# Layer 1's high halves and values stored from ScalarE's queue instead of SyncE's

## The chip, the cores and the metric

The kernel runs on one core of one Trainium2 chip. A core has five engines with instruction streams of their own: TensorE (PE), VectorE (DVE), ScalarE (ACT), GpSimd (POOL) and SyncE (SP). A DMA is issued by an instruction in one of these streams and then carried out by the core's 16 DMA engines. An engine takes its instructions in order, so an instruction that waits for a semaphore holds up all that stand behind it in the same stream. The metric is the device time of one execution in microseconds (us). The runs are given with their median; a profile belongs to one execution.

## The reference, cut to what matters

A network of two layers on x of shape (2, 512, 512), all in float32. Both layers have the form

```python
h = _layernorm(x) * (1 + ca) + sa
x = x + ga * attention(h)
h = _layernorm(x) * (1 + cb) + sb
x = x + gb * ffn(h)
```

Layer 0's attention is a chunked linear attention with decay (32 heads of 128, 8 key heads, chunks of 128 rows), with an RMS norm, a silu gate and an output projection; its FFN is a product with a matrix of signs, scaled. Layer 1's attention is what the change touches:

```python
xq = (x @ wq + bq).reshape(B, S, 32, 16)
xk = (x @ wk + bk).reshape(B, S, 8, 16)
xv = (x @ wv + bv).reshape(B, S, 8, 16)
q, k = _rope(xq, cos, sin), _rope(xk, cos, sin)
k, v = jnp.repeat(k, 4, axis=2), jnp.repeat(xv, 4, axis=2)
scores = jnp.einsum('bqhd,bkhd->bhqk', q, k) / 4
out = jnp.einsum('bhqk,bkhd->bqhd', softmax(scores), v)
```

Layer 1's FFN mixes four streams of 128 by a 4 x 4 matrix per row, which 50 Sinkhorn iterations make doubly stochastic.

## The kernel before

**Precision.** Large products run in three passes: a float32 operand is split into a high half (rounded to the fp32r type) and a low half (the rest), and `passes` (L248 to 255) adds high x high, high x low and low x high in one PSUM tile. The high half is made by a cast on ACT, the low half mostly by a subtraction on POOL, so the low half is always later than the high one.

**Who sets the order.** The kernel's text gives each operation's engine; the order in which each engine runs its instructions is found when the kernel is built, by a scheduler that plays the program through in a model of the timing and takes what is ready by priority (`schedule_with_timeline_sim=True`, L1587). An edit of one queue can so move instructions on all engines. Tiles come from pools with a fixed number of buffers, and a new use of a buffer waits for the last reader of the old one. Before the change every DMA of the kernel is issued by SP. Each DMA reports its end on one of eight semaphores, taken in turn; a DMA that takes a semaphore again waits for the earlier DMA on it, eight issues before.

**Stages.** Layer 0 is worked through in 64 units of one key head, batch and chunk. For each unit SP loads a row of decay sums into all partitions (`gb<-g_dram`, L530, one per unit), POOL masks the differences (`dec<-gb`, L532), ACT takes their exponential (L79) and DVE multiplies (L545) them into the scores. Of the rest of a unit these names occur below: `v` (L499) and `xw` (L559) weigh the values, `qh` and `ql` (L490, L491) are the halves of the queries, `yps` (L585) and `z` (L595) the outputs, `gps` and `pps` products with the gate and query weights, whose halves are `wg_h`, `wg_l` and `wq_h`, `wq_l`.

Layer 1 begins for batch 0 while layer 0's units of batch 1 are still running: `tail(n)` (L726 to 763) is called after each unit and does, by the distance c from the batch's last unit, the first norm, layer 0's FFN, the second norm, and at c = 8, 10 and 12 the projections that the change touches. They run at about 818 to 911 us for batch 0 and 1040 to 1079 us for batch 1.

**The stores.** `biased` (L695 to 698) is a projection with its bias, an ACT pass at L697. `rope_halves` (L700 to 713) turns it: `rot` is a shuffle on DVE, the products are on POOL (L705) and DVE (L706), the sum on DVE or POOL; the cast to `hi` is on ACT (L709), the subtraction for `lo` on POOL (L711), and both are stored in DRAM (L713). `project_kv` (L717) does this for the keys and stores the values (L719), `project_q` (L721) for one of four tiles of queries. Each store moves 128 x 512 float32, 256 KB. Per batch there are one value store, a high and a low one of the keys, and four high and four low ones of the queries: eleven stores, 22 in both batches.

**Who reads them.** The detour through DRAM brings the heads into another partition layout. `keys1` (L827 to 836) loads `ks` from `k_dram` (L834), `queries1` (L838 to 854) loads `qs` from `q_dram` (L849), a high row block and a low one, and `values1` (L858 to 871) loads `vT` from `v_dram` (L860), which PE transposes (`vps`, L863). All of these loads are issued by SP and wait for the stores that they read. The scores `s<-ks,qs` (L899) then run on PE, DVE takes the maxima of each row (L903), PE and ACT turn those (L917, L922) and SP writes them as extra rows into `qs` (L923); a second product (L937) gives the shifted scores, ACT their exponential `pt` (L79), and PE the weighted values `op` (L957). Layer 1's gate and norm rows are loaded at L1004 and L1012; L1117 transposes the FFN's input (`xpt`). The Sinkhorn iterations (`iterations`, L1183) run on POOL and DVE and end the kernel.

Of the kernel before, what the change touches and what calls it, by code (L numbers as in the profile page):

```python
# [9 lines left out]
FP = mybir.dt.float32  # L10
# [33 lines left out]
H1, KV1, D1 = 32, 8, 16  # L44
# [9 lines left out]
def tile_adaln(ctx: ExitStack, tc: tile.TileContext, a: dict, out: bass.AP):  # L54
    nc = tc.nc
# [116 lines left out]
    def temp(shape, dt, name, bufs=2):  # L172
        return wk.tile(shape, dt, name=name, bufs=bufs)
# [205 lines left out]
    for kc in range(KC):  # L379
# [13 lines left out]
        out=upto, in_=all1, pattern=[[1, P]], compare_op=ALU.is_ge, fill=0.0, base=0, channel_multiplier=-1,  # L393
# [73 lines left out]
    def project(n, hh, b):  # L467
        hi, lo = W[n, hh]
        ps = bank([P, L], "pps")
        passes(ps, [((hi[:, kc * P:(kc + 1) * P], lo[:, kc * P:(kc + 1) * P]), hcol(b, kc)) for kc in range(KC)])  # L470
        return ps
# [223 lines left out]
    def biased(n, t, i, b):  # L695
        raw = temp([P, L], FP, "raw1")
        nc.scalar.activation(raw, project(n, t, b), AF.Identity, bias=l1c["bias"][:, i:i + 1])  # L697
        return raw

    def rope_halves(n, t, i, b, dst):  # L700

        raw = biased(n, t, i, b)
        rot = temp([P, L], FP, "rot1")
        nc.vector.stream_shuffle(rot, raw, [j ^ 8 for j in range(32)])
        nc.gpsimd.tensor_tensor(raw, raw, l1c["rope"][0], ALU.mult)  # L705
        nc.vector.tensor_tensor(rot, rot, l1c["rope"][1], ALU.mult)  # L706
        (nc.gpsimd if RA else nc.vector).tensor_tensor(raw, raw, rot, ALU.add)
        hi = temp([P, L], FR, "hi1")
        nc.scalar.copy(hi, raw)  # L709
        lo = temp([P, L], FR, "lo1")  # L710
        nc.gpsimd.tensor_tensor(lo, raw, hi.bitcast(FP), ALU.subtract)  # L711
        for src, r in ((hi, 0), (lo, D1)):
            nc.sync.dma_start(out=dst[:, r:r + D1, :], in_=src.bitcast(FP))  # L713

    v_dram = [dram.tile([P, L], FP, name=f"v_dram{b}") for b in range(B)]

    def project_kv(b):  # L717
        rope_halves("wk1", 0, 4, b, k_dram[b])
        nc.sync.dma_start(out=v_dram[b], in_=biased("wv1", 0, 5, b))  # L719

    def project_q(b, t):  # L721
        rope_halves("wq1", t, t, b, q_dram[b][8 * t:8 * t + 8])
# [3 lines left out]
    def tail(n):  # L726
# [4 lines left out]
        for b in range(B):  # L731
# [25 lines left out]
            if c == 8:  # L757
                l1c["there", b] = True
                project_kv(b)
                project_q(b, 0)  # L760
                project_q(b, 1)
            elif c in (10, 12):
                project_q(b, c // 2 - 3)
# [697 lines left out]
    for n, u in enumerate(units):  # L1461
        g, b, c = u["at"]
# [128 lines left out]
```

## Time and profile before

| | us |
|---|---|
| median of three runs | 1349.3 |
| the runs | 1343.13, 1349.3, 1351.8 |
| the profiled execution | 1342.29 |
| its span | 1340.5 |
| stores of layer 1, batch 0, on SP | 818.3 to 911 |
| stores of layer 1, batch 1, on SP | 1049 to 1079 |

The span is the time between the first and the last instruction of the profiled execution; 1.8 us lie around it. The mean granted clock of PE was 0.969 of full speed.

The page gives the busy time of each engine and then cuts the span into 40 slices of 33.5 us; each digit is the busy share of a slice in tenths, and 9 stands for 90% or more. The row PEclk is the clock that PE was granted. In the groups of instructions each row has a line of the kernel, an engine, an operation, output and inputs, the count, the summed busy time, the mean of one in ns, and the idle time of the engine just before with what ended it:

```profile
L903 DVE TENSOR_REDUCE m<-s 128x1 f32<-128x512 f32 x256 | 165.7, 670 | 12.4 <-PE s L899 11.8
L532 POOL TENSOR_SCALAR_AFFINE_SELECT dec<-gb 128x512 f32<-128x512 f32 x64 | 47.0, 734 | 93.3 <-DMA gb<-g_dram 46.0
L254 PE MATMUL gps<-wg_h,hh 128*128 128x512 f32 x256 | 101.0, 395 | 0.7 <-DVE st L574 0.7
```

DMA-issuing instructions are not counted as busy; they appear in the timeline as rows of the queue that issues them (SPq for SP). A view of waits lists, for each engine and line, what it waited for, the time in total, how often and the longest.

All DMAs of the execution moved 109.68 MB, a mean of 82 GB/s, and one queue carried nearly all of it:

```profile
q1 hardware_dynamic: 69640, 108.21, 26.6%
q8 instruction: 57, 0.93, 0.3%
q14 instruction: 65, 0.53, 0.1%
```

The columns are packets, megabytes, and the time of the packets as a share of the 16 engines' span. The issues of the stores themselves, by line (ns minimum, median and maximum, then the first and last start in us):

```profile
L713 SPq DMA_DIRECT2D q_dram<-hi x8: 577/586/625, 832.3 to 1076.8; - x8
L713 SPq DMA_DIRECT2D q_dram<-lo x8: 575/588/620, 834.8 to 1078.4; - x8
L713 SPq DMA_DIRECT2D k_dram<-hi x2: 626/662/697, 819.2 to 1052.7; - x2
L719 SPq DMA_DIRECT2D v_dram<-raw x2: 338/340/343, 818.3 to 1049.0; - x2
```

### The profile page before, as it was taken

To read this page: it belongs to the slowest core of one execution; us is meant where nothing else is said; L and a number is where in the kernel's file an instruction comes from. 1 tells how busy PE (TensorE), PEld (TensorE's weight loads), DVE (VectorE), ACT (ScalarE), POOL (GpSimd) and SP (SyncE) were. 2 spreads that over 40 slices of the span, in tenths; PEclk is the share of its full clock that TensorE was granted. 3 is DMA by queue.
4 is the path that set the end of the run, shared out by engine and by line. 5 is a ranking of instruction groups with operands and counts; after the bars stand their busy time and mean duration, and the time that the engine had idled before them with its cause. 6 is when DMAs were issued, how large, how long until landed. Compare 5 with 4: busy or idle time off the path is not lost. (4 is left out here: it accounts for less than half of the span.)

```text
span 1340.5 us, 23011 instructions
## 1 busy us (share of the span) xinstructions
PE 1227.8 (92%) x7216; PEld 990.3 (74%) x7216; DVE 1090.6 (81%) x2665; ACT 842.1 (63%) x2375; POOL 790.9 (59%) x1233
## 2 busy tenths in 40 slices
PE   6999999999999999999989999898999999995508
PEld 3787887888788788888877788676777777764408
DVE  7888678777686687877989887877879889898888
ACT  4666665476466466766657675665758678775417
POOL 4446564364265367676788888535435856668751
PEclk9999999999999999999999999998999999998659
DMA  8013331231132143332343233424214221200001
GB/s 258 27 35 110 110 95 40 71 104 55 53 99 85 55 151 94 93 97 95 103 127 110 67 123 89 125 85 129 83 30 124 76 75 50 66 16 2 9 8 48
DMA packets 69762, 109.68 MB, mean 82 GB/s; under 512 B 13436, under 2 KB 20348, under 8 KB 69640
## 3 DMA queue, kind: packets, MB, share of 16 engines
q1 hardware_dynamic: 69640, 108.21, 26.6%
q8 instruction: 57, 0.93, 0.3%
q14 instruction: 65, 0.53, 0.1%
HBM read 99.89 MB, written 8.02 MB: 80 GB/s over the span
## 5 line engine op out<-in xcount | busy, mean ns | idle before, releaser
L903 DVE TENSOR_REDUCE m<-s 128x1 f32<-128x512 f32 x256 | 165.7, 670 | 12.4 <-PE s L899 11.8
L79 ACT ACTIVATE pt<-s 128x512 f32<-128x512 f32 x256 | 137.8, 601 | 12.2 <-PE s L937 11.2
L484 POOL TENSOR_TENSOR q<-xcos,rot 128x512 f32<-128x512 f32 x64 | 95.7, 1495 | 36.6 <-DVE xcos L482 32.9
L79 ACT ACTIVATE sg<-sg 128x512 f32<-128x512 f32 x128 | 80.9, 632 | 55.5 <-DVE sg L515 53.6
L899 PE MATMUL s<-ks,qs 96*128 96x512 f32 x256 | 103.7, 433 | 9.3 <-DVE m L903 7.5
L79 ACT ACTIVATE dec<-dec,room 128x128 f32<-128x128 f32 x256 | 82.9, 398 | 43.2 <-POOL dec L532 43.0
L254 PE MATMUL pps<-hh,wq_h 128*128 128x512 f32 x256 | 102.2, 399 | 0.8 <-DVE zl L608 0.8
L532 POOL TENSOR_SCALAR_AFFINE_SELECT dec<-gb 128x512 f32<-128x512 f32 x64 | 47.0, 734 | 93.3 <-DMA gb<-g_dram 46.0
L254 PE MATMUL ops<-wo_h,zl 128*128 128x512 f32 x256 | 100.9, 394 | 1.0 <-DVE zl L608 0.9
L254 PE MATMUL ops<-wo_h,zh 128*128 128x512 f32 x256 | 101.2, 396 | 0.7 <-DVE zl L608 0.7
L254 PE MATMUL gps<-wg_h,hh 128*128 128x512 f32 x256 | 101.0, 395 | 0.7 <-DVE st L574 0.7
L937 PE MATMUL s<-qs,ks 100*128 100x256 f32 x512 | 98.8, 299 | 1.9 <-ACT pt L79 1.4
L254 PE MATMUL gps<-wg_l,hh 128*128 128x512 f32 x256 | 100.5, 393 | 0.0
L254 PE MATMUL pps<-hl,wq_h 128*128 128x512 f32 x256 | 100.3, 392 | 0.0
L254 PE MATMUL pps<-hh,wq_l 128*128 128x512 f32 x256 | 100.2, 391 | 0.0
L254 PE MATMUL ops<-wo_l,zh 128*128 128x512 f32 x256 | 100.1, 391 | 0.0
L254 PE MATMUL gps<-wg_h,hl 128*128 128x512 f32 x256 | 100.1, 391 | 0.0
L595 DVE SCALAR_TENSOR_TENSOR z<-yps,ss,sg 128x128 f32<-128x128 f32 x256 | 71.8, 340 | 31.1 <-ACT ss L79 30.7
L552 POOL TENSOR_TENSOR gb<-gb,q 128x512 f32<-128x512 f32 x48 | 63.8, 1331 | 55.6 <-ACT gb L79 46.4
L585 PE MATMUL yps<-v,dec 128*128 128x128 f32 x512 | 93.0, 277 | 3.1 <-DVE xcos L482 2.8
L937 PEld LDWEIGHTS s<-qs,ks 100*128 100x128 f32 x512 | 82.2, 193 | 18.2 <-ACT pt L79 5.4
L559 POOL TENSOR_TENSOR xw<-v,room 128x512 f32<-128x512 f32 x48 | 57.2, 1205 | 64.7 <-ACT v L499 61.8
(331 smaller groups left out, 3901.7 us busy)
## 6 DMA issues: line engine op xcount, KB each, us to landing
gb<-g_dram SPq DMA_DIRECT2D x64, 256.0 KB
raw<-in_wq SPq DMA_DIRECT2D x56, 256.0 KB
raw<-in_wg SPq DMA_DIRECT2D x48, 256.0 KB
raw<-in_wo SPq DMA_DIRECT2D x48, 256.0 KB
raw<-in_wmod SPq DMA_DIRECT2D x40, 256.0 KB
qs<-q_dram SPq DMA_DIRECT2D x64, 64.0 KB
raw<-in_wk SPq DMA_DIRECT2D x14, 256.0 KB
raw<-in_wv SPq DMA_DIRECT2D x14, 256.0 KB
```

The costliest lines, as they stand in the source:

```text
L79: ins = nc.scalar.activation(o, i, func, **kw)
L254: nc.tensor.matmul(ps, lhsT=l, rhs=r, start=i == 0, stop=i == n - 1)
L484: nc.gpsimd.tensor_tensor(dst, sp(xc_), sp(rot), ALU.add)
L532: anchor["pool"] = nc.gpsimd.affine_select(out=dec, in_=gb, pattern=[[0, REP0], [1, P]], compare_op=ALU.is_ge, fill=-1e30, base=0, channel ...
L552: nc.gpsimd.tensor_tensor(gb, gb, q[:, c], ALU.mult)
L559: nc.gpsimd.tensor_tensor(xw, u["v"][:, c, :].unsqueeze(1).to_broadcast(sh4), wdc[:, c, r0:r0 + REP0].unsqueeze(2).to_broadcast(sh4), ALU. ...
L585: nc.tensor.matmul(yps[:, h, :], lhsT=u["pr"][:, h, :], rhs=u["v"][:, c, :], start=True, stop=not c)
L595: nc.vector.scalar_tensor_tensor(z[:, h, :], yps[:, h, :], ss[:, h:h + 1], sg[:, h * P:(h + 1) * P], ALU.mult, ALU.mult)
L899: anchor["pe"] = nc.tensor.matmul(ps, lhsT=st["qs"][rp][0:KS, i, qt * P:(qt + 1) * P], rhs=st["ks"][s][0:KS], start=True, stop=True,).ins
L903: anchor["dve"] = nc.vector.tensor_reduce(st["m"][:, 2 * qt + s, i:i + 1], ps, AX.X, ALU.max, negate=True).ins
L937: nc.tensor.matmul(ps[:, j, :], lhsT=st["ks"][s][0:KM, kt * P:(kt + 1) * P], rhs=st["qs"][rp][0:KM, i, :], start=True, stop=True,)
```

## The change

The stores of the high halves and of the values are issued by ACT. The low halves stay with SP, and so do all loads.

```diff
@@ -709,14 +709,14 @@
         nc.scalar.copy(hi, raw)
         lo = temp([P, L], FR, "lo1")
         nc.gpsimd.tensor_tensor(lo, raw, hi.bitcast(FP), ALU.subtract)
-        for src, r in ((hi, 0), (lo, D1)):
-            nc.sync.dma_start(out=dst[:, r:r + D1, :], in_=src.bitcast(FP))
+        for src, r, queue in ((hi, 0, nc.scalar), (lo, D1, nc.sync)):
+            queue.dma_start(out=dst[:, r:r + D1, :], in_=src.bitcast(FP))
 
     v_dram = [dram.tile([P, L], FP, name=f"v_dram{b}") for b in range(B)]
 
     def project_kv(b):
         rope_halves("wk1", 0, 4, b, k_dram[b])
-        nc.sync.dma_start(out=v_dram[b], in_=biased("wv1", 0, 5, b))
+        nc.scalar.dma_start(out=v_dram[b], in_=biased("wv1", 0, 5, b))
 
     def project_q(b, t):
         rope_halves("wq1", t, t, b, q_dram[b][8 * t:8 * t + 8])
```

Of the 22 stores twelve move: per batch the values, the keys' high half and four high halves of queries.

## The prediction

> **What bounds the kernel now.** I read the page's busy times first, then its slices, then the waits of TensorE (PE), then the timeline of each engine around PE's longest wait. Busy times and slices:
>
> ```profile
> PE 1227.8 (92%) x7216; PEld 990.3 (74%) x7216; DVE 1090.6 (81%) x2665; ACT 842.1 (63%) x2375; POOL 790.9 (59%) x1233
> PE   6999999999999999999989999898999999995508
> DVE  7888678777686687877989887877879889898888
> PEclk9999999999999999999999999998999999998659
> ```
>
> PE is the bound up to slice 36. The last four slices (1206 to 1340 us) are the tail of Sinkhorn passes, where DVE is busy 117.59 of 134 us and PE 66.92. The changed stores are issued between 818 and 1078 us. So the question is how early PE gets through its work; the tail then follows as it stands. PE's idle time by stretch (window, its length, PE busy; after the five engines the granted clock):
>
> ```profile
> 838.00:871.00 33.00, 29.33 (x130) 22.19 (x131) 28.93 (x53) 20.20 (x57) 17.86 (x16) 1.00 0.43 124
> 871.00:904.50 33.50, 30.65 (x169) 25.67 (x169) 25.48 (x56) 20.44 (x58) 11.99 (x12) 1.00 0.27 87
> 918.00:923.10 5.10, 0.10 (x1) 0.00 (x0) 3.65 (x4) 5.10 (x12) 4.10 (x4) 0.98 0.34 96
> 923.10:930.00 6.90, 5.94 (x21) 4.70 (x22) 6.68 (x13) 4.37 (x10) 2.62 (x5) 0.52 0.57 167
> 1049.00:1080.00 31.00, 28.41 (x194) 22.52 (x192) 28.93 (x67) 20.70 (x51) 25.16 (x37) 0.94 0.40 109
> 1080.00:1206.00 126.00, 125.41 (x1157) 93.36 (x1159) 112.05 (x347) 99.41 (x245) 75.94 (x313) 1.00 0.18 48
> ```
>
> Idle in these from 838 to 1080: 3.67 + 2.85 + 5.00 + 0.96 + 2.59 = 15.1 us. After the 5 us stop the clock is 0.52 for 6.90 us: 6.90 x 0.48 = 3.3 us more lost. So some 18.4 us is all that better timing could win near these stores. What ended the waits of PE and of SyncE (SP):
>
> ```profile
> PE s L899 <- DVE m L903: 7.5, 5, 5.0
> PE vps L863 <- DVE rot L476: 2.5, 1, 2.5
> PE xpt L1117 <- ACT raw L697: 1.9, 1, 1.9
> SPq L713 <- ACT ss L79: 12.8, 1, 12.8
> ```
>
> The last is 12.8 us in which SP's queue stood behind one store of a high half, up to 905.7. The timelines say what that cost (start, duration, engine and line; in brackets the idle time):
>
> ```profile
> 905.71 0.62 SPq L713 DMA_DIRECT2D q_dram<-hi  x1
> 909.78 0.80 SPq L849 DMA_DIRECT2D qs<-q_dram  x2
> 910.62 0.62 SPq L713 DMA_DIRECT2D q_dram<-lo  x1
> 911.34 0.39 SPq L530 DMA_DIRECT2D gb<-g_dram  x1
> 916.45 0.64 POOL L532 TENSOR_SCALAR_AFFINE_SELECT dec<-gb 128x512 f32<-128x512 f32 x1 [4.17 <-PE ztp L603]
> 917.12 1.28 ACT L79 ACTIVATE dec<-dec,room 128x128 f32<-128x128 f32 x4 [8.71 <-POOL dec L532]
> 923.13 0.79 PE L899 MATMUL s<-ks,qs 96*128 96x512 f32 x1 [5.03 <-DVE m L903]
> ```
>
> The high half was stored at 905.71, the query load behind it waited until 909.78, the low half went at 910.62 and only then the decay rows gb at 911.34. gb landed some 5.1 us later (916.45 on POOL, idle for 4.17 us); ACT (8.71 us idle), then DVE and PE followed, PE at 923.13 with 5.03 us lost. The releaser named for PE is only the last link.
>
> **The change, part by part.** It removes twelve issues from SP and adds twelve on ACT's queue; arithmetic, bytes and destinations are the same. In a comparison of the two programs' instruction lists the scheduler has also reordered PE's rows of about 836 to 930, 1053 to 1110 and 1165 to 1200 us; elsewhere the lists agree or shuffle the tail with equal counts.
>
> (a) *The gb stop.* In the new list SP no longer waits for this high half. But gb still follows the low half, the same tile's POOL subtraction, which cannot start before the high half's cast. In the old trace the cast ended at 905.69 and the subtraction ran from 907.06 for 1.28 us, behind two POOL multiplications of 2.05 us; the new list puts it ahead of those. So it is ready near 906.3 to 906.9 and gb is issued near 907, not 911.34: 4.4 us earlier. All of PE's 5.03 us can go that way; I take -4.4, bounds -5.0 and 0 (0 if SP is held by another wait). Next late is DVE, busy 3.65 of those 5.10 us, which is why I don't take the full 5. With a stop under 1 us the low clock should mostly vanish: 0 to -3.3, taken -2.0, since 1.9 and 2.5 us waits elsewhere show 0.94 or 1.00 and not 0.52.
>
> (b) *Values, first batch.* PE waited 2.5 us at the value transposes (L863); their load was issued at 833.44, behind a high store at 832.31. The new list has the load right behind the key loads, about 1.5 us earlier. -1.5, bounds -2.5 and 0.
>
> (c) *The issues on ACT.* No ACT-issued DMA is in this trace. Nearest rows: SP's issues of these very stores, median 586 ns x8 (q), 662 x2 (k), 340 x2 (v): 4.7 + 1.3 + 0.7 = 6.7 us. ACT is busy 63% of the span, so most of it lies in idle ACT time: 13 us of 33 idle in 838 to 871. Ends: 0 and 6.7. It is on the path where PE waits for ACT: a store now stands between a layer-1 bias pass (L697) and the products that feed xpt (L1117), where PE already waits 1.9; +0.6 there, and as much again at one or two of the other eleven, +1.5 in all. Below nothing is excluded for the issue itself; its removal from SP is costed in (a), (b) and (d). A store sits right behind its own cast, or behind one to six more ACT instructions, so the wait for its data is short. Each DMA also waits for an older DMA on one of eight shared completion semaphores; those named in ACT's list were finished by the old times (the latest issued at 1068.4 on SP against about 1076), so 0; if one isn't, ACT stands still for one landing, 4 to 6 us by the rows above.
>
> SP's head waited up to 12.8 us while an issue takes 0.6: by these rows, what is at stake is the position in the queue, not the issue. [...]
>
> (d) *Second batch on SP.* The low half stored at 1074.98 stands in the new list ahead of four query loads, issued at 1071.39 before. They go at about 1075.5, 4 us later, and land about 5 us after that, at 1080.5, against the product that reads them at 1078.9. Cost 0 to +2; I take +0.5, as PE has other rows in that stretch to fill in.
>
> (e) *Reordered rows.* Same work, other gaps. This can't be worked out from rows; 0, bounds -8 and +8: the gaps left in 838 to 1080 after (a) and (b), 18.4 - 7.9 = 10.5, could largely close, or one stop like the old one could open (5.0 + 3.3 = 8.3).
>
> Sum: -4.4 - 2.0 - 1.5 + 1.5 + 0.5 + 0 = -5.9 us. The profiled execution took 1342.29 us (1340.5 of span, 1.8 around it), 7.0 below the median of the runs, 1349.3. So 1336.4 for such an execution, and 1343.4 for a median. All three runs lie within 0.7%: a change under 1% (13.5 us) can't well be told from none.
>
> **Rivals.**
> *The wait only passes from hi to lo.* SP stands before the low half instead; the scheduler's order puts the gb load no earlier in fact. For: SP's order keeps lo ahead of gb. Against: the landing wait of the query loads (909.78) is no longer between. Price: terms (a), (b) gone, (c) and (d) left: +2, 1351.
>
> *The gaps close.* Reordering and freed SP close all 18.4 us: 1331. For: by the same view SP stood behind ACT for 9.9, 7.7 and 12.8 us from 804 to 960. Against: the 10.5 us outside (a), (b) have other releasers.
>
> *Slower: ACT in its order becomes what PE waits for.* Place: the stage from 838 to 938, where PE's next operand comes over ACT casts (ACT is busy all 5.10 us of 918 to 923.1). A store queued there before such casts delays them by its 0.6 us, or by a landing if its shared semaphore is still out. It decides once the cast is later than PE's work at hand, as at 923.13: then a stop of 5.0 and a low clock of 3.3, beside 6.7 of issues, and without the gains of (a), (b): +15, 1364. Against: ACT has idle time, and the list shows no semaphore that should be late.
>
> **How the numbers follow.** Forecast 0.40 (own range 1336 to 1349: from all of (a) and (b), 10.8, with 2.5 of (e), to nothing won); wait passed on 0.12; gaps close 0.22; slower 0.26, this high because a new order on four engines can open stops that I can't see in the old trace. The predicted time is the forecast's, 1343. The range goes from 1331 to 1363: it leaves out half of each outer case, 0.11 + 0.13 at most, less what lies between them and the forecast. Faster by over 1% (under 1335.8): the gaps' 0.22 and 0.03 of the forecast's edge, 0.25; slower by over 1% (above 1362.8): 0.26; within: 0.49.
>
> **What would show it.** Right: PE's 5.03 us before L899 gone or under 1 us, no stretch at clock 0.52 near 923, gb issued within 2 us of lo's subtraction, the 12.8 us wait of SP gone or now ending at lo, twelve issues of about 0.6 us on ACT. PE's stretch to 1206 ends some 6 us earlier with an unchanged tail. Wrong: a new PE wait over 3 us between 838 and 930 that ends at an ACT cast or at an ACT-issued store; ACT waiting at L713 for a DMA; the query loads of the second batch late by more than 2 us; or a longer tail.

## The result and the profile after

| | before | after |
|---|---|---|
| median, us (17 runs each) | 1350.02 | 1353.46 |
| lowest and highest | 1342.47, 1352.7 | 1349.41, 1357.1 |
| the profiled execution, its span | 1342.29, 1340.5 | 1357.1, 1355.4 |
| mean granted clock of PE in it | 0.969 | 0.953 |

The ratio is 1.0032, 95% interval 1.0018 to 1.0047: the change costs about 0.3%, where some 0.4% less time had been forecast. The two profiled executions are 15 us apart, far more than the medians. The one of before lies 7.7 us below its median and the one of after 3.6 above; 4.1 of the 15 us arise in the first 120 us, where both kernels have the same instruction lists. So a difference of single profiles is worth something only in one stretch of work, and only if other executions repeat it.

From the page of after (busy time of each engine; the granted clock in 40 slices of 33.9 us; the DMA queue that is new):

```profile
PE 1243.9 (92%) x7216; PEld 1003.3 (74%) x7216; DVE 1089.0 (80%) x2665; ACT 842.3 (62%) x2375; POOL 786.5 (58%) x1233
PEclk9999999999999999999999999988999999997659
q10 hardware_dynamic: 1648, 3.15, 0.8%
```

The counts are those of before. 3.15 MB, twelve stores of 256 KB, are now in a queue of their own. PE has 16.1 us more of busy time for the same 7216 products, which is not more work. At the lower clock products took longer (in E9, below, those of 512 columns follow one another every 0.43 us near 887 us, at half clock, and every 0.23 near 912, at full clock), and the clock was lower: ahead of the tail it is below 9 tenths in two slices, from 881 to 949 us, where before had one. 7.5 of the 16.1 us lie in the stretch shown below.

The issues of ACT by line (ns minimum, median, maximum):

```profile
L713 ACTq DMA_DIRECT2D q_dram<-hi x8: 583/587/595, 837.2 to 1089.8; - x8
L713 ACTq DMA_DIRECT2D k_dram<-hi x2: 601/878/1155, 823.8 to 1063.1; - x2
L719 ACTq DMA_DIRECT2D v_dram<-raw x2: 321/336/352, 823.2 to 1059.4; - x2
```

By these medians the twelve take 7.1 us, against 6.7 forecast. Now the stretch of the old 5 us stop, in the timeline of after:

```profile
916.26 1.29 POOL L711 TENSOR_TENSOR lo<-raw,hi 128x512 fp32r<-128x512 f32 x1 [4.54 <-ACT hi L709]
917.58 0.63 SPq L713 DMA_DIRECT2D q_dram<-lo  x1
918.30 0.41 SPq L530 DMA_DIRECT2D gb<-g_dram  x1
923.78 0.64 POOL L532 TENSOR_SCALAR_AFFINE_SELECT dec<-gb 128x512 f32<-128x512 f32 x1 [3.87 <-DMA gb<-g_dram]
925.64 1.05 POOL L559 TENSOR_TENSOR xw<-v,room 128x512 f32<-128x512 f32 x1
926.64 1.29 POOL L484 TENSOR_TENSOR q<-xcos,rot 128x512 f32<-128x512 f32 x1
927.96 1.14 ACT L490 CAST qh<-q 128x512 fp32r<-128x512 f32 x2 [1.20 <-POOL q L484]
928.62 2.79 DVE L491 TENSOR_TENSOR ql<-q,qh 128x512 fp32r<-128x512 f32 x2 [3.15 <-ACT qh L490]
931.33 1.27 DVE L903 TENSOR_REDUCE m<-s 128x1 f32<-128x512 f32 x2
932.06 0.68 PE L899 MATMUL s<-ks,qs 96*128 96x512 f32 x1 [2.75 <-DVE m L903]
```

gb is issued 0.75 us after lo's subtraction ends. By the clock that is 7.0 us later than before, but PE is 11 us behind in its list here, so gb comes some 4 us earlier against the work. PE's stop went from 5.03 only to 2.75 us: POOL's product q, behind its weighing xw, and ACT's cast of it are late next; DVE stands 3.15 us for that cast, and the maxima m that PE needs are behind its ql.

To see where the time went, each execution is cut at the same products of PE's list. This is the stretch that reaches from 830 to 960 us in before, and inside it the part of before's 860 to 905 (window, length, PE busy and count, weight loads, DVE, ACT, POOL, granted clock, DMA share, GB/s). Before:

```profile
830.00:960.00 130.00, 115.67 (x649) 91.84 (x647) 105.91 (x202) 78.51 (x208) 66.12 (x60) 0.97 0.38 110
860.00:905.00 45.00, 41.12 (x213) 33.02 (x212) 36.41 (x78) 26.69 (x78) 18.54 (x18) 1.00 0.24 73
```

After, at the same products:

```profile
833.80:970.50 136.70, 123.21 (x648) 97.24 (x647) 104.11 (x203) 79.58 (x216) 65.54 (x59) 0.91 0.36 107
864.90:913.70 48.80, 44.29 (x212) 33.34 (x215) 36.58 (x75) 25.13 (x70) 17.61 (x17) 0.90 0.22 68
```

6.7 us more for the same 649 products; idle time is a little less (13.5 against 14.3) and the clock is 0.91 instead of 0.97. More than half of it, 3.8 us, lies in 860 to 905, before the old stop, where before had a clock of 1.00. What PE waited for in this stretch of after (total, times, longest):

```profile
PE s L899 <- DVE m L903: 4.3, 3, 2.7
PE cps L254 <- DVE xcos L482: 3.5, 1, 3.5
PE ops L254 <- DVE dec L545: 2.8, 1, 2.8
```

The last two waits stand in no row of before for this stretch.

### The profile page after: what moved, and what is told of

It reads as the page before. It is cut to its first block, busy times and chain, and to the rows that moved or that the text cites. A ratio compares the mean times of both kernels' runs of the same rounds, so it can differ in the third digit from the quotient of the medians.

```text
span 1355.4 us, 22993 instructions
## 1 busy us (share of the span) xinstructions
PE 1243.9 (92%) x7216; PEld 1003.3 (74%) x7216; DVE 1089.0 (80%) x2665; ACT 842.3 (62%) x2375; POOL 786.5 (58%) x1233
## 3 DMA queue, kind: packets, MB, share of 16 engines
q10 hardware_dynamic: 1648, 3.15, 0.8%
## 4 chain that ended last, share of the span: by engine, by line
PE 63%; DVE 16%; POOL 7%; issue 5%; DMA 4%; ACT 3%; SPq 1%; POOLq 0%; DVEq 0%; ACTq 0%
PE pps L254 15%; PE ops L254 10%; PE gps L254 10%; PE op L957 4%; PE s L937 4%; PE s L899 3%; PE yps L585 3%; PE sps L254 2%; PE yps L587 2%; PE cps L254 2%; PE mps L293 2%; PE ztp L603 1%; DVE m L903 1%; POOL q L484 1%; DVE sinkhorn L1211 1%
## 5 line engine op out<-in xcount | busy, mean ns | idle before, releaser
L79 ACT ACTIVATE pt<-s 128x512 f32<-128x512 f32 x256 | 138.0, 600 | 18.8 <-PE s L937 12.4
L484 POOL TENSOR_TENSOR q<-xcos,rot 128x512 f32<-128x512 f32 x64 | 92.4, 1445 | 40.5 <-DVE xcos L482 39.2
L899 PE MATMUL s<-ks,qs 96*128 96x512 f32 x256 | 104.9, 438 | 6.6 <-DVE m L903 4.6
L559 POOL TENSOR_TENSOR xw<-v,room 128x512 f32<-128x512 f32 x48 | 55.3, 1165 | 62.1 <-ACT v L499 59.3
```

Of the source, the lines that this page charges most:

```text
L79: ins = nc.scalar.activation(o, i, func, **kw)
L484: nc.gpsimd.tensor_tensor(dst, sp(xc_), sp(rot), ALU.add)
L559: nc.gpsimd.tensor_tensor(xw, u["v"][:, c, :].unsqueeze(1).to_broadcast(sh4), wdc[:, c, r0:r0 + REP0].unsqueeze(2).to_broadcast(sh4), ALU. ...
L899: anchor["pe"] = nc.tensor.matmul(ps, lhsT=st["qs"][rp][0:KS, i, qt * P:(qt + 1) * P], rhs=st["ks"][s][0:KS], start=True, stop=True,).ins
```

## The experiments

**Holding an order.** The change does two things at once: it moves twelve issues, and the scheduler makes another order on four engines. To part them, a kernel is built with a stored list of instruction names for each engine; behind the last operation, dependencies that set an order and nothing else are added between neighbours of the list:

```diff
+    traced = {i.name: i for i in nc.cur_bb.bb.instructions}
+    for steps_ in json.loads(zlib.decompress(base64.b85decode(ORDER))).values():
...
+            if last is not None:
+                tc.add_manual_dep(m, last.name, order_only, reason="the order held")
+            last = m
```

The tiles' places in SBUF are laid out anew by each build, so they are a third thing that can differ (2192 of 3819 places moved between before and E1). All ratios below are against runs of the kernel before on the same chip.

### E1 to E4: queue and order apart

Four kernels: the stores on SP or on ACT (the diff of the change), each with the order of before or of after. Where the stores are on the other queue than in the kernel that the order comes from (E2 and E3, later E6, E7 and E15), the twelve stores themselves are not in the stored list, and the scheduler places them.

> Stores on SP as before; the order of each engine's instructions is held, by order-only dependencies, to that of the kernel before. The tiles get other addresses in SBUF (2192 of 3819), since the packing is done anew. Control for the next three. Theory A (the slowdown comes from the new order of instructions): within 0.2% of the kernel before. Theory B (it comes from ACT carrying twelve DMA issues): within 0.2% of before. Theory C (it comes from where tiles lie, since a tile that takes over the place of a stored one waits for the store to land): off by 0.3% or more, either way, because the places are shuffled here and nothing else is.

> Twelve stores on ACT as in the change, but PE, DVE, POOL, and ACT's and SP's other instructions held to the order of before. Theory A: no slower than the control with SP (within 0.2% of it), perhaps faster by up to 0.4% since the stop of 5.0 us before L899 loses its cause on SP. Theory B: slower than the control by 0.3% (3 to 4 us). Theory C: differs from the control by its own places, no sign forecast.

> Stores on SP as before, but all engines held to the order that the changed kernel has. Theory A: slower than before by about 0.3%, like the changed kernel. Theory B: like before. Theory C: no sign forecast.

> The changed kernel with its own order held, other addresses. Theory A and theory B: 0.3% slower than before, like the changed kernel. Theory C: may be anywhere within 0.5%.

| | order of before | order of after |
|---|---|---|
| stores on SP | E1 1349.60, 0.9998 [0.9984, 1.0012] | E3 1355.52, 1.0049 [1.0031, 1.0067] |
| stores on ACT | E2 1345.50, 0.9980 [0.9964, 0.9996] | E4 1353.51, 1.0029 [1.0013, 1.0046] |

The new order costs 0.5% with either queue (E3 less E1, E4 less E2); the queue alone brings 0.2% with either order, which is within the intervals. E1 repeats before and E4 repeats after, so neither holding an order nor the places moved the time measurably. The change is slower for its reordered rows, not for anything that ACT or SP does with the stores.

What kind of time is it? For each execution: the length of the stretch above, PE's idle time in it, the time lost in stretches at half clock, where PE was granted 0.50 (as an estimate, half of PE's busy time there, added up from the records), and the rest.

| order | kernel | length | idle | low clock | rest |
|---|---|---|---|---|---|
| of before | before | 130.0 | 14.3 | 2.9 | 112.8 |
| | E1 | 132.8 | 15.7 | 4.1 | 112.9 |
| | E2 | 131.0 | 13.0 | 5.5 | 112.5 |
| | E6 (below) | 131.0 | 13.0 | 5.5 | 112.5 |
| of after | after | 136.8 | 13.5 | 10.7 | 112.6 |
| | E3 | 138.0 | 15.7 | 9.3 | 113.0 |
| | E4 | 136.1 | 15.2 | 7.3 | 113.6 |
| | E5 (below) | 136.5 | 14.4 | 7.9 | 114.1 |

The means are 131.2 and 136.9: 5.7 us more in the new order, of which 0.7 is idle time, 4.3 low clock and 0.6 the rest. That agrees with the 5.9 us between the medians of E1 and E3. By parts, three executions each (before, E1, E2 against after, E3, E4): 860 to 905 takes 45.5 and 49.1 us, 905 to 960 takes 55.7 and 57.1, what lies ahead 30.1 and 30.8.

### E5 and E9: a subtraction that waits for a store

In the profiles of after, E3 and E4 PE stops for 2.8, 3.7 and 4.3 us at the output projection (`ops`), always for DVE's `dec`. In E4, by the timeline:

```profile
859.64 0.58 SPq L713 DMA_DIRECT2D q_dram<-lo  x1
864.18 0.69 DVE L491 TENSOR_TENSOR ql<-q,qh 128x512 fp32r<-128x512 f32 x1 [3.16 <-DMA q_dram<-lo]
864.79 0.86 DVE L545 SCALAR_TENSOR_TENSOR dec<-sps,room,dec 128x128 f32<-128x128 f32 x3
865.80 0.77 PE L254 MATMUL ops<-wo_h,zh 128*128 128x512 f32 x1 [4.33 <-DVE dec L545]
```

The buffer that ql is written to held a half that was being stored, and it came free only when the store had landed, 4.5 us after its issue. DVE stands there 3.16 us, with the products `dec` behind it that PE needs. In after it is the high half stored by ACT at 862.92, whose semaphore ql waits for, and ql starts at 867.03 (the view names POOL's `w_l`, which ended within 0.1 us of that). In E3 ql waits only 0.58 us; there ACT's cast qh stands first, for a high half that SP stored at 860.86, and DVE waits 3.63 us at a `dec` that comes after it:

```profile
864.85 0.62 ACT L490 CAST qh<-q 128x512 fp32r<-128x512 f32 x1 [2.93 <-DMA q_dram<-hi]
```

So it happens with either queue: in the new order a writer meets a buffer that is still being stored, and what PE needs stands behind that writer. E5 moves ql behind the three dec, E9 further behind zl (L608), which PE needs too (in DVE's list, the stores on ACT as in E4):

```diff
-ql L491, dec L545 x3, ..., zl L608, rot x2, m x3
+dec L545 x3, ql L491, ..., zl L608, rot x2, m x3          (E5)
+dec L545 x3, ..., zl L608, rot x2, m x3, ql L491          (E9)
```

> The changed kernel with its own order held, but one DVE instruction moved: the subtraction that makes ql of the next queries (L491) goes behind the three decay multiplications (L545) that stood after it, near 865 us. Theory A1 (the order costs because ql waits at DVE's head for its buffer, and PE waits for the multiplications behind it): PE's wait before the products ops, 2.8 to 4.3 us, falls under 1 us, the low clock after it goes, and the kernel is 4 to 6 us faster than the changed one with its order held (1353.5), so near 1348. Rival A2 (something else is as late): within 1.5 us of 1353.5.

> As the changed kernel with its order held, but DVE's subtraction for ql (L491) goes further back: behind the decay multiplications, the gate and zl (L608), two rotations and three maxima. Theory A1 (DVE stands still for a stored tile to land, since ql got that tile's place, and the items behind ql are what PE needs): PE's waits at 855 to 870 us fall from 3 to 4 us to under 1.5 in all, the low clock near 885 goes, 5 to 6 us faster than 1353.5: 1347.5 to 1349. Rival A2 (the loss of that stretch has another cause, as moving ql by three places changed nothing): within 1.5 us of 1353.5.

E5: 1356.1, 1.0039 [1.002, 1.0059], no gain on E4. The forecast gain of 4 to 6 us did not come. The wait only passed on to zl, which now stood behind ql, by the timeline of E5:

```profile
861.73 0.58 SPq L713 DMA_DIRECT2D q_dram<-lo  x1
866.12 0.69 DVE L491 TENSOR_TENSOR ql<-q,qh 128x512 fp32r<-128x512 f32 x1 [2.20 <-DMA q_dram<-lo]
867.06 0.74 DVE L608 SCALAR_TENSOR_TENSOR zl<-ztp,room,zh 128x512 fp32r<-128x512 f32 x1
867.86 0.58 PE L254 MATMUL ops<-wo_h,zl 128*128 128x512 f32 x1 [3.09 <-DVE zl L608]
```

E9: 1351.8, 1.003 [1.0012, 1.0047], the ratio of E4 again, although the stop at ops fell from 4.33 to 1.10 us. The stretch got only 0.8 us shorter (135.3 against 136.1), as a half-clock stretch of 6.8 us from 882.8 was still there. Taking the wait away alone is worth nothing that can be measured.

### E13 and E14: the row of short products

That half-clock stretch is in every profile of the new order in which PE's list was not edited: from 887.8 in after (granted 0.50 up to 894.6), 882.4 in E4, 885.2 in E5 and 883.8 in E10, 6.8 us each, 3.4 us in E3. Of the old order's, before, E1 and E8 have none there; E2 and E6 have 3.4 us near 877 to 880 and E7 at 868. What PE runs ahead of it, in E9:

```profile
877.22 0.71 PE L899 MATMUL s<-ks,qs 96*128 96x512 f32 x2
877.77 0.40 PE L937 MATMUL s<-qs,ks 100*128 100x256 f32 x2
878.16 0.51 PE L899 MATMUL s<-ks,qs 96*128 96x512 f32 x1
878.82 0.50 PE L937 MATMUL s<-qs,ks 100*128 100x256 f32 x2 [0.15 <-DVE zl L608]
879.93 1.10 PE L899 MATMUL s<-ks,qs 96*128 96x512 f32 x2 [0.61 <-DVE m L903]
881.05 0.51 PE L937 MATMUL s<-qs,ks 100*128 100x256 f32 x2
881.65 1.09 PE L899 MATMUL s<-ks,qs 96*128 96x512 f32 x2
...
883.44 1.39 PE L899 MATMUL s<-ks,qs 96*128 96x512 f32 x2
```

PE is called busy almost throughout, but each score product L899 has to wait for DVE's maximum of an earlier one (0.67 us, the mean in before). From 877.22 to 883.44 it got through 7 products of 512 columns, 6 of 256 and 2 of 128 (in the row left out), together as much as 10.5 of 512. At full clock long products follow one another every 0.23 us (in E9 near 912), so by an estimate 27 of them fit in these 6.2 us: PE streamed some 0.4 of that. In this part of before's list no more than six score products L899 come between two groups of long ones; in the new order it is ten, one ahead of yps and nine behind it. E13 puts the next twelve long products (the projection of layer 0's values, `wv_h` and `wv_l`, 512 columns) four at a time between them, on top of E9; E14 does it on E4, with ql where it was. In PE's list:

```diff
-yps, L899 x2, L937 x2, L899, L937 x2, L899 x2, L937 x2, L899 x2, ..., ttp, wv x12
+yps, wv x4, L899 x2, L937 x2, L899, L937 x2, wv x4, L899 x2, L937 x2, wv x4, L899 x2, ..., ttp
```

> The order of the changed kernel with ql moved back, and on PE the twelve long products of the values' projection (pps, 512 columns) that followed the row of short products are put between them, four at a time, behind yps and two pairs of L937. Theory D (in the new order the score products L899, whose maxima DVE takes at 0.6 us each, stand in a row with yps, ztp and mt, PE streams only a third of the time there, and the clock falls to half for 6.8 us near 885): the low clock near 885 goes or halves, 3 to 5 us faster than with ql alone moved (1351.8): 1347 to 1349. Rival E (the row is not what lowers the clock, or the products wait for something else): within 1.5 us of 1351.8.

> The same without moving ql. Theory D: the low clock near 885 goes, the wait at ql (2.8 to 4.3 us) stays: 2 to 4 us faster than the changed kernel's order (1353.5), 1350 to 1351.5. Rival E: 1353.5 +- 1.5.

E13: 1349.34, 0.9996 [0.998, 1.0012], level with before. Its PE in the same place:

```profile
877.11 0.48 PE L254 MATMUL pps<-hh,wv_h 128*128 128x512 f32 x1
...
878.11 0.63 PE L899 MATMUL s<-ks,qs 96*128 96x512 f32 x2
...
883.33 0.62 PE L899 MATMUL s<-ks,qs 96*128 96x512 f32 x2
```

A pair of L899 takes 0.62 us at 883.33, against 1.39 at 883.44 in E9: the clock stays up. The same work of the part 860 to 905, in E9:

```profile
861.50:909.10 47.60, 43.84 (x212) 32.42 (x214) 36.57 (x75) 25.25 (x70) 16.95 (x17) 0.92 0.21 69
```

and in E13:

```profile
862.40:905.00 42.60, 39.88 (x212) 29.90 (x214) 36.26 (x74) 24.78 (x68) 16.52 (x16) 1.00 0.24 76
```

5.0 us less, with the clock at 1.00; 4.0 of them are PE's busy time for the same 212 products, 1.0 is idle time. The whole stretch from 830 takes 131.3 us, as in the old order (131.2 on the mean). E14: 1352.45, 1.0027 [1.001, 1.0044]. Its profile has no low clock there either and its stretch is 2.3 us shorter than E4's, but the stop at ops is 2.54 us, and the median is that of E4 within its interval. Only both edits together bring the kernel level with before. Against E2, which has the old order with the same queue (0.9980), 0.16% of the order's 0.49% are left, which is within the intervals. Why E14's gain shows in the profile and not in its median is open.

### E6: which of the reordered places

The order also differs from 1053 to 1110 and 1165 to 1200 us. E6 has the stores on ACT, the order of before up to PE's 4300th instruction, which is behind the stretch above, and then that of after:

```diff
-ORDER: before's lists
+ORDER: before's lists up to PE's instruction 4300, then after's
```

> Stores on ACT; the order of before up to a point behind the first batch's stores (PE instruction 4300 of 5944, between 940 and 1040 us), from there the order of the changed kernel. If the loss lies in the first batch's stretch alone: like stores on ACT with the order of before, 1345.5 +- 1.5. If the second batch's new order costs too: 1347 to 1350.

1350.97, 1.0002 [0.9983, 1.002], between E2 (0.9980) and E4 (1.0029) with intervals that overlap E2's. Its stretch of 830 to 960 takes 131.0 us, as in E2. The trace shows a stop of 1.29 us at `ot` (1076.28) that E2 lacks, and 6.8 us at half clock from 1030.3, where E2 has 3.4 from 1027.9 with the same order there. By matched products, the work of before's 1049 to 1115 us takes 0 to 2.0 us more than in before in the executions that have the old order there (before, E1, E2, E7, E8) and 1.4 to 3.8 us more in nine that have the new one (after, E3 to E6, E9, E10, E13, E14): by the means, an estimate of 1.5 us from single executions. So the first batch carries the larger part; whether the second adds 0.2% or nothing was not settled by the medians.

### E7, E8 and E10: the gb stop by itself

In E2, with the high half on ACT but the old order, gb was issued at 911.95 and PE stopped for 4.86 us: SP stood at the query loads, which wait for that store to land, instead of at the store. What holds gb there is the kernel's own rule: `gated` (L150 to 160) keeps a unit's gb load behind SP's work beside an earlier unit. E7 (ACT) and E8 (SP) lift it for SP and set gb ahead, of the query loads and of the high store; the rest of before's order is held. E10 does the like on E9, ahead of the last low store.

```diff
         for e, m in anchor.items():
-            if e != "free" and m.name not in past:
+            if e not in ("free", "sp") and m.name not in past:
```

> Stores on ACT, the order of before, and one SP instruction moved: the load of the decay rows gb that came after the low half's store (911.95 us in the run without this) goes ahead of the two query loads that wait for a store to land. Theory (the 5 us stop of PE before L899 is made by gb's place in SP's queue): the stop falls under 1.5 us, the low clock after it goes too, 5 to 8 us faster than without it, 1338 to 1341. Rival (another input is as late): at most 1.5 us faster, 1344.

> Stores on SP, the order of before, and the same load of gb moved ahead of the high half's store and the query loads. By the same theory the stop goes without any change of queue: 5 to 8 us faster than with the order of before (1349.6), 1342 to 1345. Rival: at most 1.5 us faster.

> The same, and SP's load of gb goes ahead of the last low half's store of the first batch. If the rest of the 5 us stop, 2.75 us and the low clock behind it, hangs on gb alone: 3 to 5 us faster than the run with ql alone moved. If POOL's other work is as late: at most 1.5 us.

E7: 1343.12, 0.9959 [0.9937, 0.9982]. E8: 1343.78, 0.9949 [0.993, 0.9968]. The timeline of E8:

```profile
899.62 0.33 SPq L530 DMA_DIRECT2D gb<-g_dram  x1
...
922.23 0.72 PE L899 MATMUL s<-ks,qs 96*128 96x512 f32 x2 [0.88 <-DVE m L903]
```

gb goes some 12 us earlier than in before, the stop is 0.88 us, and behind it PE is at half clock for 3.4 us (from 924.3) instead of 6.8. The stretch from 830 takes 126.0 us, against 130.0 in before and 132.8 in E1, with 10.5 us idle and 1.6 lost to the low clock (3.4 in E7, which has a second such stretch at 868). This gain of 0.4 to 0.5% was there all along and needs no other queue; E7 and E8 differ by 0.1%. E8's gain on E1, 0.5%, is what was forecast; E7's on E2 is 0.2%, between the forecast and its rival, and why is open. E10: 1351.68, 1.0026 [1.0007, 1.0046]. Its stop fell only from 2.98 to 2.14 us. In the new order gb is no longer what is late: POOL's next q waits 1.32 us for DVE's xcos, and ACT's cast and ql follow it.

### E11, E12 and E15: versions

E11 and E12 have only the edit of `gated` above, with the scheduler free, on before (SP) and on after (ACT). E15 is E11's order held with the stores on ACT.

> The kernel before with one edit and no order held: the loads of gb are no longer told to keep behind the other SP work of an earlier unit. Stores on SP. The scheduler puts the late gb ahead of the high half's store by itself, and reorders some of PE, DVE and ACT. If gb's place is the main thing: like the held order with gb ahead, 1343.8 +- 2. If the new order opens a stop like that of the change: 1348 to 1352.

> The changed kernel with the same edit and no order held; ql no longer has the place of a stored tile in its list of places. If that place and gb's position were what cost: 1342 to 1346, faster than before and than the changed kernel. If stores on ACT cost by themselves or the order does so elsewhere: 1349 or more.

> Stores on ACT with the order of the fast kernel that lets gb go freely (1341.6 with stores on SP). If the queue alone is worth 0.2% and shortens the wait at the value transposes (4.5 us there) as it did with the order of before: 1337 to 1340. If the queue is worth nothing or costs there: 1341.5 or more.

E11: 1341.58, 0.9957 [0.9937, 0.9977], the lowest median of all and faster than both kernels, with the stores left on SP (by the ratios E7, E8 and E11 can't be told apart). E12: 1350.85, 1.0019 [0.9997, 1.0041]; it again got another order, and its longest waits are 3.3 us at `cps` and 2.6 at the scores. E15: 1345.87, 0.997 [0.9956, 0.9985]. ACT's queue took PE's wait for vT from 4.53 to 0.92 us, but 7 us later PE waited 2.52 us for qs instead. So there are four pairs that differ in the queue alone, ACT less SP: -0.18% (E2, E1), -0.20% (E4, E3), +0.10% (E7, E8), +0.13% (E15, E11). In each pair the intervals overlap: the queue by itself is worth nothing that these runs can tell from none.

## Why the prediction was wrong

The sign was wrong: -5.9 us forecast, +3.4 measured. By its steps:

**(e) failed.** "Reordered rows ... 0, bounds -8 and +8": the new order costs 5.9 us in the medians (E3 less E1) and 8.0 with ACT (E4 less E2), up to the edge of these bounds. It was put at 0 because no row gave it, and it proved the largest term. Its two parts in the first batch are shown together, by E13 (1.0029 to 0.9996): an instruction that stands until a store's buffer is free, in E4 a subtraction on DVE for 3.16 us, and a row of short products: over the part of 860 to 905 the clock is 0.92 with it (E9) and 1.00 with long products between (E13). Either one taken away alone (E9, E14) left the median where it was. Neither can be read from the old trace alone; but the new list was known, and the row of ten L899 with no long product between them stood in it.

**(a) was right in mechanism and too large.** gb came 4 us earlier against the work, as worked out. (By its own rows the term was a little high: the cast's end at 905.69, 1.28 us for the subtraction and some 0.7 for the issue of lo ahead of gb put gb at 907.7, 3.6 us earlier, not 4.4.) But only 2.28 of the forecast 4.4 us came off PE's stop, since POOL's q and ACT's cast were late next, not DVE, and the low clock behind it, -2.0 forecast, stayed: 6.8 us at half clock from 932.2, as in before. From 905 to 960 the new order is 1.4 us longer, not 6.4 shorter. Nor did the queue bring gb forward: in E2 it did not move.

**(b) had the wrong releaser.** The wait at the values was put down to their load. By the old timeline it was a rotation on DVE:

```profile
832.31 0.58 SPq L713 DMA_DIRECT2D q_dram<-hi  x1
...
837.57 0.69 DVE L475 TENSOR_TENSOR rot<-pps,rope 64x512 f32<-64x512 f32 x1 [1.73 <-DMA q_dram<-hi]
...
839.00 0.63 PE L863 MATMUL vps<-room,vT 128*128 128x128 f32 x4 [2.52 <-DVE rot L476]
```

The rotation takes the buffer of the stored high half: the same mechanism as in E5. With other places the load does end it (3.54 us in E1, 4.53 in E11), and there ACT's queue makes it short (0.15 in E2, 0.92 in E15). In after, PE does not wait there, but 3.5 us for xcos near 845 (4.2 in E3, 1.2 in E4).

**(c) was too dear.** The issues take 0.587 us as forecast, but cost nothing that shows: PE's wait at xpt is 1.84 us against 1.89 of before, and the queue's effect in four orders lies between -0.2 and +0.1%. A stop of 1.44 us for the bias pass (L697) at `ot` in the second batch is new; E3, with the stores on SP, has 0.55 there, so a small cost in this place is not excluded.

**(d) was nothing.** PE has no wait for the late query loads.

**The rivals.** "Slower" had the sign, at four times the price (+15), but the wrong mechanism: no cast of ACT in after waited behind a store for long; it was the order. (Casts that waited for a store to land, 2.93 and 2.4 us, are in E3, with the stores on SP.) "The wait passes from hi to lo" was half seen: SP now waits 25.5 us in six stands for lo's subtraction (longest 8.8), and this costs PE little. "The gaps close" is refuted for this change (its sum of 18.4 us, called all that could be won, also left out 3.1 us of idle time from 938 to 1049); part of that gain is what E8 and E11 take.

What stays open: why the scheduler chose the new order, how far the second batch matters, and why neither of the two edits pays by itself.

## What to carry to other kernels

Where a scheduler sets the order, an edit of a queue is an edit of every engine's order: build both orders with both queues before anything is said about the queue. Look in the new list for the first reuse of a buffer whose last reader is a store (here 4.0 to 5.3 us from the store's issue to the next writer), and for a row of products that each wait for another engine; put long independent products between those (that part took 47.6 us in E9 and 42.6 in E13). When a load is late, ask first which rule or dependency holds it in its place: moving that one load was worth 0.4 to 0.5%, moving twelve stores nothing.

## What was not expected of the hardware

PE's clock fell while PE counted as busy. From 876 to 893 us PE is busy for 15.68 of 17 us in E4 and 15.97 in E13, and the granted clock is 0.80 and 1.00. What differs is how densely PE works: the worth of 10.5 of 27 possible long products around the fall in E9; in E13, counted in the same way from 877.11 to 883.33, 17 products of 512 columns and 6 of 256, that is 20 of 27. The low stretches near there last 3.4 or 6.8 us at half clock. It was no long gap that came ahead: the longest in the 5.6 us ahead of the fall in E9 is 0.61 us.

The clock did not fall in every thin row. In before the row from 872.85 to 879.28 (six score products of 512 columns, eight products of 256 and six of 128, with a gap of 2.69 us among them) is worth 11.5 of 28 possible long products, as thin as the row in E9, and the clock stayed at 1.00. In before and in after all changes of the clock lie on one grid of 3.41 us (in after, 870.8, 887.8 and 932.2 are 5 and 13 steps apart); whether it matters how the work falls into these steps was not shown. Of the 15 long products that fit in one at 0.23 us each, PE streamed the worth of 5 in the step ahead of the fall in E9 and of 4.5 to 5.5 in after, E3, E4, E5 and E10; in before it was 7, 7.5 and 9 in the steps from 871.7 on. That is no sharp limit: E2, E6 and E7 fell after 5.5 to 6.5, and before kept its clock after 5.5 (from 861.5). What decides was not measured.

Here a store held its buffer for long: 4.5 us from the issue on SP to the first writer of the same place in E4, 4.4 in E5, 4.0 in E3, 4.1 in after with ACT as the issuer, 5.3 in before, for 256 KB whose issue takes 0.6 us.
